# A relational graph layer: who fetches the message rows, which engine copies, and how wide the one-hot products are

## The chip, the cores and the metric

The kernel runs on one core of a Trainium2 chip. The metric is the device time of one execution in microseconds (us), the median of several runs. A core has five engines with instruction queues of their own: TensorE (PE), VectorE (DVE), ScalarE (ACT), GpSimd (POOL) and SyncE (SP). Each works through its queue in order, and semaphores tie them together. Transfers are issued by SP, ACT or POOL and carried out by DMA engines.

## The reference

There are N = 12500 nodes with 256 features and E = 212500 edges, sorted by destination, among them one loop edge per node, which is the last edge of its node. Each edge has one of R = 8 types.

```python
h = jnp.maximum(_layernorm(x, axis=-1), 0.0)
hx = jnp.einsum('ni,rio->rno', h, weight)            # (8, 256, 256) weights
agg = jax.ops.segment_sum(hx[edge_type, src], dst, num_segments=num_nodes)
node_repr = agg * 0.5 ** 0.5 + h_bias
return x + node_repr + (h @ loop_weight) * 0.5 ** 0.5
```

## The kernel before

The kernel first sums rows of h per destination and type, and multiplies by the weights afterwards, once per node and type.

**Norms.** In the first 110 us SP loads x in pieces of 512 rows, DVE and ACT normalise them, and SP writes h to a table in DRAM. Edges taken before that table is complete have rows of x gathered instead, which DVE and ACT normalise in place (kind "x").

**Units and tiles.** Edges are taken in 802 units. The first 128 units (block 0) hold 256 edges each. Later units hold 267 edges, from which the loop edges are squeezed out, so that at most 256 are left. Each unit is two tiles of 128 edges, 1603 tiles in all. Blocks of 128 units are prepared together on DVE (`prepare`): source numbers (`gidx`), window columns (`col`), and, for some tiles, source addresses in bytes (`single`). Which half of a unit a tile holds is told by `place_of`.

**Gathers.** For tile t, `gather` (L739) puts an indirect DMA on POOL's queue (L755): 128 rows of 1 KB into a buffer `msg`, one edge per partition. It is put down AHEAD = 58 tiles before the tile is used; there are 60 tile buffers, in pairs. Every SINGLE-th tile (t%48 = 47, from block 1 on) is not gathered by POOL: `load_sources` (L759) loads 16 addresses into registers of SP (L762), and SP then issues one DMA per row (L767). The list `fetches` spreads these steps: it begins HOLD = 8 tiles after the tile was put down, and `fetch` takes FETCH = 4 of them per tile.

**Sums.** DVE builds one-hot matrices (L785), 176 columns per edge: 22 window nodes times 8 types. PE multiplies rows by one-hots (L818), two matrix products per tile, each as two matmuls of fp32, and adds a unit's two tiles in one PSUM bank. REACH gives offset and width, in nodes, of each tile's window: 22 nodes for the first tile of a unit (176 columns), 18 from node 4 on for the second (144 columns). `add_sums` (L832, DVE) adds the bank to a ring of accumulators `acc` in SBUF, at an offset in a register. There are four banks.

**Nodes.** Groups of 128 nodes follow when their sums are complete: 32 matmuls with the weights plus 4 with the loop weight (L1009), spread over the tiles by a planner that counts DVE credits, then two additions (L1021, L1022) and an output store by SP (L1027). For a group to come, PE turns rows of h into `pt` (L859), DVE writes the loop edges' part of the accumulators (L881, eight operations), and ACT copies `pt` to `self_t` (L864). Every fourth group, the types of the loop edges are found: marks (L902, DVE), a matmul, `kinds`, four `diagonal` products on ACT (L934), a matmul that spreads them, and a copy to `types` on ACT (L945).

The program order within each queue is written out by the Python loop over t; nothing reorders it.

Of the kernel before, what the change touches and what calls it, by code (L numbers as in the profile page):

```python
# [13 lines left out]
AF = mybir.ActivationFunctionType  # L14
ALU = mybir.AluOpType
# [3 lines left out]
SYNC_DEP = mybir.DependencyInfo(mybir.DependencyClass.Sync, mybir.DependencyReason.DATA)  # L19
DVE = mybir.EngineType.DVE  # L20
SP = mybir.EngineType.SP

P = 128
EPS = 1e-5
# [3 lines left out]
XG = 4  # L28
# [4 lines left out]


WIN = 22
REACH = ((0, 22), (4, 18))

GROUP = 128

# [4 lines left out]
MSGS = 60  # L44
AHEAD = 58

SINGLE = 48
FETCH = 4
SOURCES = 16
HOLD = 8  # L50


# [167 lines left out]
def kernel(  # L220
# [54 lines left out]

    def place_of(t):
        u, i = divmod(t, PAIR)
        return u // P, i, u % P


    with ExitStack() as main:
# [32 lines left out]
        single, fetches = {}, []  # L314
        state = {"h32": None}


# [39 lines left out]
        def kept_sources(b, got):  # L357

            def keep():
                single[b] = idx.tile([P, P], I32, name="single")  # L360
                nc.vector.tensor_single_scalar(
                    single[b], got["sf"][:, P:U], float(D * 4), op=ALU.mult)

            return [keep]

# [115 lines left out]
        def columns(b, got):  # L481


            halves = [(slice(i * P, (i + 1) * P), o, n) for i, (o, n) in enumerate(REACH)]

            def bases():
                if b == 0:
# [16 lines left out]
                        got["there"][:, h], got["col"][:, h], float(o), None, op0=ALU.is_ge)  # L504

            def plain_to():
                nc.vector.scalar_tensor_tensor(
                    got["there"][:, :U], got["col"][:, :U], float(WIN), got["there"][:, :U],
                    op0=ALU.is_lt, op1=ALU.mult)

            def plain_typed():
                nc.vector.scalar_tensor_tensor(
# [226 lines left out]
        def gather(t):  # L739
            if t % PAIR == 0:  # L740
                both = msgs.tile([P, PAIR, D], F32, name="msg")
                for i in range(PAIR):
                    msg[t + i] = both[:, i, :]
            if t % QUAD:
                kind[t] = kind[t - 1]
            else:
                kind[t] = "h" if state["h32"] is not None and t >= state["h32"] + LATE else "x"
            table = {"h": h32, "x": x}[kind[t]]
            b, i, u = place_of(t)
            if b and i and kind[t] == "h" and t % SINGLE == SINGLE - 1 and t + AHEAD < NT:  # L750
                for r in range(0, P, SOURCES):
                    fetches.append((done["tile"] + HOLD, lambda r=r: load_sources(t, r)))
                return
            at = i * P + u
            nc.gpsimd.indirect_dma_start(  # L755
                out=msg[t], out_offset=None, in_=table[:, :],
                in_offset=bass.IndirectOffsetOnAxis(ap=gidx[b][:, at : at + 1], axis=0))

        def load_sources(t, r0):  # L759

            b, _, u = place_of(t)
            _, vals = nc.values_load_multi_w_load_instructions(  # L762
                single[b][u : u + 1, r0 : r0 + SOURCES], engines=[SP],
                min_val=0, max_val=(N - 1) * D * 4,
                skip_runtime_bounds_check_because="clamped to the table where they are computed")
            for i, v in reversed(list(enumerate(vals))):
                fetches.insert(0, (0, lambda i=i, v=v: nc.sync.dma_start(  # L767
                    msg[t][r0 + i : r0 + i + 1, :].bitcast(U8),
                    h32_bytes[:, bass.ds(v, D * 4)])))

        def fetch(n):
            for _ in range(n):
                if fetches and fetches[0][0] <= done["tile"]:
                    fetches.pop(0)[1]()

        def onehots(t):

            n = min(QUAD, NT - t)
            o = ohs.tile([P, QUAD // PAIR, PAIR, C], F32, tag="oh", name="oh")
            b, _, u = place_of(t)  # L780
            k = 0
            for v, i in ((n // PAIR, PAIR), (1, n % PAIR)):
                if v and i:
                    of = col[b].rearrange("p (i u) -> p u i", i=PAIR)[:, u + k : u + k + v, :i]
                    j = nc.vector.tensor_tensor(  # L785
                        o[:, k : k + v, :i, :],
                        iota_f.unsqueeze(1).unsqueeze(1).to_broadcast([P, v, i, C]),
                        of.unsqueeze(3).to_broadcast([P, v, i, C]), op=ALU.is_equal)
                    k += v
            for i in range(n):  # L790
                oh[t + i] = o[:, i // PAIR, i % PAIR, :]
                made[t + i] = j.ins.name

        def load_offsets(u0):
# [8 lines left out]
        def edge_sums(t):  # L803
            m, o = msg.pop(t), oh.pop(t)
            if t % PAIR == 0:
                bank = banks[t // PAIR % BANKS]
                sums["ps"] = bank[:, : KC * R * WIN].rearrange("p (c k) -> p c k", c=KC)
            ps = sums["ps"]
            i = t % PAIR
            from_, width = (a * R for a in REACH[i])  # L810
            end = t == NT - 1 or i == PAIR - 1
            free = added.get(t // PAIR - BANKS)
            if i == 0 and free is not None and latest["pe"] is not None:
                tc.add_manual_dep(latest["pe"], free.name, SYNC_DEP, reason="bank is free")
            if i == 0 and latest["pe"] is not None:
                tc.add_manual_dep(latest["pe"], made[t], SYNC_DEP, reason="one-hots are made")
            for c in range(KC):
                j = nc.tensor.matmul(  # L818
                    ps[:, c, from_ : from_ + width], m[:, c * P : (c + 1) * P], o[:, :width],
                    start=(i == 0 and c == 0), stop=(end and c == KC - 1))  # L820
            latest["pe"] = j.ins
            return ps
# [28 lines left out]
        def turn_nodes(g, pool, written=None):  # L851

            n = plan.ends[g] - plan.starts[g]
            pst = pt[:, : KC * P].rearrange("p (c d) -> p c d", c=KC)

            def turn():
                rows_ = got["h", g // XG][:, g % XG, :]
                for c in range(KC):
                    nc.tensor.transpose(  # L859
                        pst[:, c, :n], rows_[:n, c * P : (c + 1) * P], ident[:n, :n])  # L860

            def keep():
                got["self", g] = pool.tile([P, KC, GROUP], F32, name="self_t")
                i = nc.scalar.activation(got["self", g][:, :, :n], pst[:, :, :n], AF.Copy)  # L864
                if written:
                    tc.add_manual_dep(
                        i.ins, written[0].name, SYNC_DEP, reason="one reader at a time")

            return turn, keep, pst

        def begin(g):

            n = plan.ends[g] - plan.starts[g]
            q, k = divmod(g, XG)
            written = []
            turn, keep, pst = turn_nodes(g, selves, written)
            s0 = g % SLOTS * GROUP

            def own(r):
                of = typed[q][:, k * GROUP : k * GROUP + n].unsqueeze(1).to_broadcast([P, KC, n])  # L880
                i = nc.vector.scalar_tensor_tensor(  # L881
                    acc[:, :, r, s0 : s0 + n], of, float(r + 1), pst[:, :, :n],
                    op0=ALU.is_equal, op1=ALU.mult)
                if r == R - 1:
                    zeroed[g, "slot"] = i.ins
                    written.append(i.ins)
# [20 lines left out]
        def find_types(q):  # L907
# [11 lines left out]
            def kinds_of():  # L919
# [27 lines left out]
            shared(spread, [(1, types_of)], lambda: q in marked, wait=2)  # L947

        got = {}

# [14 lines left out]
        def group_ahead(g):  # L965
# [11 lines left out]
            if q < plan.typed:  # L977
                def turned_nodes():
                    turn, keep, _ = turn_nodes(g, early)
                    shared(turn, [(1, keep)])  # L980

                work.append((0.4, turned_nodes))
            if k == XG - 2:
# [286 lines left out]
```

## Time and profile before

Times are in us.

| what | value |
|---|---|
| median of 3 runs | 2020.09 (2018.17 to 2021.71) |
| profiled execution: time, span | 2023.05, 2021.3 |
| PE, busy | 1796.2 |
| DVE, busy | 1317.4 |
| ACT, busy | 218.4 |
| POOL, busy | 1500.7 |
| gathers from h / from x | 1480 / 96 |
| rows fetched one by one by SP | 3456 |
| matmuls of 176 / 144 columns (L818) | 3208 / 3204 |
| granted TensorE clock, mean | 0.957 |

A group line gives source line, engine, operation, written tile <- read tiles, shape, count, then busy time and the mean duration of one. A timeline line gives start, duration, engine, line and operation, and in brackets the idle time before it with what ended it. A line of busy time by stage gives the stretch, its length, busy time with the number of instructions for PE's matmuls and weight loads, then granted clock, DMA share and GB/s. A line of waits gives who waited for whom, the total, the number and the longest. SPq is SP's sequencer, which issues DMAs. Durations under a source line are minimum/median/maximum in ns.

### The profile page before, as it was taken

How to read it: one execution, taken by the hardware profiler on the slowest of the kernel's cores; microseconds unless marked ns; L12 is line 12 of the kernel's file. 1: busy time of each engine (PE TensorE's matmuls, PEld its weight loads, DVE VectorE, ACT ScalarE, POOL GpSimd, SP SyncE). 2: the span in 40 equal slices, each digit the busy share in tenths (PEclk: the TensorE clock that was granted, in tenths of full speed). 3: DMA queues.
4: the chain of work that ended last, by engine and by line, in shares of the span. 5: the costliest groups of instructions: out<-in, count | busy, mean ns of one | idle time of the engine just before them, and what ended most of it. 6: DMA issues, size and time to landing. Idle time of an engine off the chain costs nothing.

```text
span 2021.3 us, 36386 instructions
## 1 busy us (share of the span) xinstructions
PE 1796.2 (89%) x10411; PEld 1610.0 (80%) x10411; DVE 1317.4 (65%) x3281; ACT 218.4 (11%) x470; POOL 1500.7 (74%) x1602
## 2 busy tenths in 40 slices
PE   2468999997999898999899999998998898998998
PEld 2357999997888888988788788787787787787886
DVE  7869566687656578656577655577665568665642
ACT  7854110000000000000000000000000000000000
POOL 7766777777777777777777777777777777777773
PEclk8569999998999999999999999999999999999999
DMA  8973443444444444444444444444444444444442
GB/s 296 380 222 97 146 138 106 128 138 127 129 139 118 139 137 117 130 118 139 130 126 139 128 124 135 132 122 140 129 118 138 125 123 129 118 138 123 118 120 73
DMA packets 152577, 281.63 MB, mean 139 GB/s; under 512 B 31149, under 2 KB 101940, under 8 KB 152372
## 3 DMA queue, kind: packets, MB, share of 16 engines
q0 software_dynamic: 75648, 206.67, 35.1%
q1 hardware_dynamic: 76724, 72.61, 11.4%
q8 instruction: 82, 1.34, 0.3%
q14 instruction: 123, 1.01, 0.2%
HBM read 253.55 MB, written 25.60 MB: 138 GB/s over the span
## 4 chain that ended last, share of the span: by engine, by line
PE 38%; DMA 20%; SPq 17%; issue 12%; POOL 7%; DVE 5%; ACT 2%; DVEq 0%; POOLq 0%; ACTq 0%
PE ps L818 20%; PE po L1009 17%; DMA msg<-h,gidx 13%; SPq L767 13%; POOL msg L755 7%; SPq L762 4%; DMA hr<-h 2%; DMA h<-xt 1%; DVE e_stats L701 1%; DVE acc L832 1%; ACT xt L713 1%; DMA xr<-in_x_dram 1%; DMA w<-in_L_gnn_weight_dram 1%; DMA msg<-h 1%; DVE oh L785 1%
## 5 line engine op out<-in xcount | busy, mean ns | idle before, releaser
L755 POOL DMA_INDIRECT msg<-h,gidx x1480 | 1407.7, 951 | 464.2 <-issue 371.1
L818 PE MATMUL ps<-oh,msg 128*128 128x176 f32 (+1 forms) x6412 | 1169.6, 312 | 201.5 <-DMA msg<-h,gidx 78.5
L818 PEld LDWEIGHTS ps<-oh,msg 128*128 128x128 f32 x6412 | 1037.8, 196 | 355.3 <-DMA msg<-h,gidx 159.1
L1009 PE MATMUL po<-w,acc 128*128 128x256 f32 x3136 | 883.0, 383 | 1.8 <-DVE acc L832 1.8
L832 DVE TENSOR_TENSOR acc<-acc,ps 128x352 f32 x802 | 415.1, 518 | 503.4 <-PE ps L818 499.1
L1009 PEld LDWEIGHTS po<-w,acc 128*128 128x128 f32 x3136 | 537.6, 192 | 25.3 <-DVE acc L832 2.6
L785 DVE TENSOR_TENSOR oh<-fixed,cols 128x704 f32<-128x704 f32 x402 | 353.0, 879 | 0.0
L881 DVE SCALAR_TENSOR_TENSOR acc<-types,pt 128x256 f32<-128x256 bf16 (+1 forms) x688 | 249.0, 411 | 77.5 <-PE pt L859 71.5
L864 ACT ACTIVATE self_t<-pt 128x256 f32<-128x256 f32 x98 | 37.5, 383 | 1456.4 <-DVE acc L881 1352.5
L755 POOL DMA_INDIRECT msg<-in_x_dram,gidx x96 | 91.0, 948 | 31.1 <-issue 24.4
L1009 PE MATMUL po<-wl,self_t 128*128 128x256 f32 x392 | 105.2, 391 | 4.9 <-ACT self_t L864 2.5
L1009 PEld LDWEIGHTS po<-wl,self_t 128*128 128x128 f32 x392 | 69.1, 196 | 11.4 <-ACT self_t L864 2.9
L1021 DVE TENSOR_TENSOR xr<-xr,po 128x256 f32<-128x256 f32 x98 | 40.5, 413 | 17.5 <-PE po L1009 15.7
L713 ACT ACTIVATE xt<-xt,n_shift,n_rstd 128x256 f32<-128x256 f32 x98 | 50.9, 588 | 8.6 <-DVE n_shift L710 8.6
L713 ACT ACTIVATE msg<-msg,e_shift,e_rstd 128x256 f32<-128x256 f32 x96 | 49.6, 589 | 12.8 <-DVE e_shift L710 12.8
L1022 DVE TENSOR_TENSOR xr<-xr,po 128x256 f32<-128x256 f32 x98 | 41.2, 420 | 3.4
L934 ACT ACTIVATE diagonal<-ident,kinds 128x128 bf16<-128x128 f32 x88 | 28.1, 390 | 135.0 <-DVE kinds L931 130.1
L859 PE MATMUL pt<-ident,hr 128*128 128x128 f32 x196 | 37.9, 275 | 0.0
L370 DVE TENSOR_SCALAR moves<-fixed 128x267 int32<-128x267 int32 x84 | 36.0, 428 | 1.1
L701 DVE BATCH_NORM_STATS2 n_stats<-xt 128x6 f32<-128x256 f32 x98 | 34.4, 412 | 2.5 <-DMA xt<-in_x_dram 1.7
L371 DVE COPY_PREDICATED fixed<-moves,fixed 128x266 int32<-128x266 int32 (+6 forms) x84 | 33.7, 401 | 2.9
L701 DVE BATCH_NORM_STATS2 e_stats<-msg 128x6 f32<-128x256 f32 x96 | 33.5, 411 | 0.0
(201 smaller groups left out, 319.7 us busy)
## 6 DMA issues: line engine op xcount, KB each, us to landing
msg<-h SPq DMA_DIRECT2D x3456, 1.0 KB
msg<-h,gidx POOLq DMA_INDIRECT x1480
xt<-in_x_dram SPq DMA_DIRECT2D x24, 512.0 KB
h<-xt SPq DMA_DIRECT2D x24, 512.0 KB
xr<-in_x_dram SPq DMA_DIRECT2D x24, 512.0 KB
hr<-h SPq DMA_DIRECT2D x24, 512.0 KB
out_dram<-xr SPq DMA_DIRECT2D x24, 512.0 KB
w<-in_L_gnn_weight_dram SPq DMA_DIRECT2D x2, 1024.0 KB
```

Source lines behind the costliest of these rows:

```text
L701: nc.vector.bn_stats(stats[:n, j, :], rows_[j])
L713: nc.scalar.activation(rows_[j], rows_[j], AF.Relu, bias=shift[:n, j : j + 1], scale=rstd[:n, j : j + 1])
L755: nc.gpsimd.indirect_dma_start(out=msg[t], out_offset=None, in_=table[:, :], in_offset=bass.IndirectOffsetOnAxis(ap=gidx[b][:, at : at + 1 ...
L762: _, vals = nc.values_load_multi_w_load_instructions(single[b][u : u + 1, r0 : r0 + SOURCES], engines=[SP], min_val=0, max_val=(N - 1) * D ...
L767: fetches.insert(0, (0, lambda i=i, v=v: nc.sync.dma_start(msg[t][r0 + i : r0 + i + 1, :].bitcast(U8), h32_bytes[:, bass.ds(v, D * 4)])))
L785: j = nc.vector.tensor_tensor(o[:, k : k + v, :i, :], iota_f.unsqueeze(1).unsqueeze(1).to_broadcast([P, v, i, C]), of.unsqueeze(3).to_broa ...
L818: j = nc.tensor.matmul(ps[:, c, from_ : from_ + width], m[:, c * P : (c + 1) * P], o[:, :width], start=(i == 0 and c == 0), stop=(end and ...
L832: i = nc.vector.tensor_tensor(a, a, ps, op=ALU.add)
L881: i = nc.vector.scalar_tensor_tensor(acc[:, :, r, s0 : s0 + n], of, float(r + 1), pst[:, :, :n], op0=ALU.is_equal, op1=ALU.mult)
L1009: i = nc.tensor.matmul(got["out", g][:n], lhs, rhs, start=(r == R and c == 0), stop=(r == R - 1 and c == KC - 1))
L1021: nc.vector.tensor_add(rows_[:n, k, :], rows_[:n, k, :], outs[g % 2][:n, 1, :])
L1022: nc.vector.tensor_add(rows_[:n, k, :], rows_[:n, k, :], got["out", g][:n])
```

## The change

It does these things:

- SINGLE goes from 48 to 32, so that one tile in 32 is fetched row by row. Its rows are shared: runs of 32 rows (SOURCES) go in turn to SP and ACT, each with a list of its own, and FETCH = 3 steps per tile are taken from each list.
- `self_t` and `types` are copied by DVE instead of ACT, and the four `diagonal` products on ACT become one operation on DVE. The extra dependency that kept ACT behind DVE's last reader of `pt` goes.
- The two halves of a unit change places: PE takes the second half of the edges first, at 176 columns, and then the first half, in a window of 13 nodes from node 0 (104 columns, before 144). In the last block both halves have 176 columns.

```diff
+ACT = mybir.EngineType.Activation
-REACH = ((0, 22), (4, 18))
+REACH = ((0, 13), (0, 22))
-SINGLE = 48
-FETCH = 4
-SOURCES = 16
+SINGLE = 32
+FETCH = 3
+SOURCES = 32
     def place_of(t):
         u, i = divmod(t, PAIR)
-        return u // P, i, u % P
+        half = 0 if PAIR * u + 1 == NT else PAIR - 1 - i
+        return u // P, half, u % P
...
-                    single[b], got["sf"][:, P:U], float(D * 4), op=ALU.mult)
+                    single[b], got["sf"][:, :P], float(D * 4), op=ALU.mult)
...
-            if b and i and kind[t] == "h" and t % SINGLE == SINGLE - 1 and t + AHEAD < NT:
-                for r in range(0, P, SOURCES):
-                    fetches.append((done["tile"] + HOLD, lambda r=r: load_sources(t, r)))
-                return
+            if b and t % PAIR and kind[t] == "h" and t + AHEAD < NT:
+                if t % SINGLE == SINGLE - 1:
+                    for k, r in enumerate(range(0, P, SOURCES)):
+                        engine = (SP, ACT)[k % 2]
+                        fetches[engine].append((
+                            done["tile"] + HOLD,
+                            lambda r=r, engine=engine: load_sources(t, r, engine)))
+                    return
...
         def fetch(n):
-            for _ in range(n):
-                if fetches and fetches[0][0] <= done["tile"]:
-                    fetches.pop(0)[1]()
+            for list_ in fetches.values():
+                for _ in range(n):
+                    if list_ and list_[0][0] <= done["tile"]:
+                        list_.pop(0)[1]()
...
-            from_, width = (a * R for a in REACH[i])
+            width = R * (REACH[0][1] if i and t // (PAIR * P) < NB - 1 else WIN)
...
-                    ps[:, c, from_ : from_ + width], m[:, c * P : (c + 1) * P], o[:, :width],
+                    ps[:, c, :width], m[:, c * P : (c + 1) * P], o[:, :width],
...
-                i = nc.scalar.activation(got["self", g][:, :, :n], pst[:, :, :n], AF.Copy)
-                if written:
-                    tc.add_manual_dep(
-                        i.ins, written[0].name, SYNC_DEP, reason="one reader at a time")
+                nc.vector.tensor_copy(got["self", g][:, :, :n], pst[:, :, :n])
...
-                for g in range(XG):
-                    nc.scalar.activation(
-                        marked[q][:, g * GROUP : (g + 1) * GROUP], ident, AF.Copy,
-                        scale=kinds[:, g : g + 1])
+                nc.vector.tensor_tensor(
+                    marked[q].rearrange("p (g k) -> p g k", g=XG),
+                    ident.unsqueeze(1).to_broadcast([P, XG, GROUP]),
+                    kinds.unsqueeze(2).to_broadcast([P, XG, GROUP]), op=ALU.mult)
...
-                nc.scalar.activation(typed[q], pt, AF.Copy)
+                nc.vector.tensor_copy(typed[q], pt)
```

The copies of `types` and of the first groups' `self_t` are also placed one tile later in the program. The preparation of window columns follows the new REACH; it writes one more operation for block 0.

More of the change, by code (lines that the diff above doesn't have):

```diff
@@ L313 @@
         added, zeroed = {}, {}
-        single, fetches = {}, []
+        single, fetches = {}, {SP: [], ACT: []}
         state = {"h32": None}
@@ L481, in columns @@
         def columns(b, got):
-            halves = [(slice(i * P, (i + 1) * P), o, n) for i, (o, n) in enumerate(REACH)]
+            halves = [(slice(i * P, (i + 1) * P), o, n)
+                      for i, (o, n) in enumerate(REACH if b < NB - 1 else ((0, WIN), (0, WIN)))]
             def bases():
@@ L506, in plain_to @@
             def plain_to():
-                nc.vector.scalar_tensor_tensor(
-                    got["there"][:, :U], got["col"][:, :U], float(WIN), got["there"][:, :U],
-                    op0=ALU.is_lt, op1=ALU.mult)
+                for h, o, n in halves:
+                    nc.vector.scalar_tensor_tensor(
+                        got["there"][:, h], got["col"][:, h], float(o + n), got["there"][:, h],
+                        op0=ALU.is_lt, op1=ALU.mult)
             def plain_typed():
@@ L757, in gather, with load_sources @@
                 in_offset=bass.IndirectOffsetOnAxis(ap=gidx[b][:, at : at + 1], axis=0))
-        def load_sources(t, r0):
+        def load_sources(t, r0, engine):
             b, _, u = place_of(t)
             _, vals = nc.values_load_multi_w_load_instructions(
-                single[b][u : u + 1, r0 : r0 + SOURCES], engines=[SP],
+                single[b][u : u + 1, r0 : r0 + SOURCES], engines=[engine],
                 min_val=0, max_val=(N - 1) * D * 4,
                 skip_runtime_bounds_check_because="clamped to the table where they are computed")
+            queue = {SP: nc.sync, ACT: nc.scalar}[engine]
             for i, v in reversed(list(enumerate(vals))):
-                fetches.insert(0, (0, lambda i=i, v=v: nc.sync.dma_start(
+                fetches[engine].insert(0, (0, lambda i=i, v=v: queue.dma_start(
                     msg[t][r0 + i : r0 + i + 1, :].bitcast(U8),
@@ L790, in onehots @@
             for i in range(n):
-                oh[t + i] = o[:, i // PAIR, i % PAIR, :]
+                oh[t + i] = o[:, i // PAIR, place_of(t + i)[1], :]
                 made[t + i] = j.ins.name
@@ L849, in clear, with turn_nodes @@
             zeroed[g, "slot"] = i.ins
-        def turn_nodes(g, pool, written=None):
+        def turn_nodes(g, pool):
             n = plan.ends[g] - plan.starts[g]
@@ L874, in begin @@
             q, k = divmod(g, XG)
-            written = []
-            turn, keep, pst = turn_nodes(g, selves, written)
+            turn, keep, pst = turn_nodes(g, selves)
             s0 = g % SLOTS * GROUP
@@ L885, in own @@
                     zeroed[g, "slot"] = i.ins
-                    written.append(i.ins)
             def write():
@@ L944, in types_of @@
                 typed[q] = types.tile([P, XG * GROUP], BF16, name="types")
-                nc.scalar.activation(typed[q], pt, AF.Copy)
-            shared(spread, [(1, types_of)], lambda: q in marked, wait=2)
+                nc.vector.tensor_copy(typed[q], pt)
+            shared(spread, [(2, types_of)], lambda: q in marked, wait=2)
         got = {}
@@ L979, in turned_nodes @@
                     turn, keep, _ = turn_nodes(g, early)
-                    shared(turn, [(1, keep)])
+                    shared(turn, [(2, keep)])
                 work.append((0.4, turned_nodes))
```

## The prediction

> **What bounds the kernel now.** I read the page's shares first, then instructions by shape, GpSimd's timeline, busy time by stage, and the waits. The shares of the page name no bound:
>
> ```profile
> PE 1796.2 (89%) x10411; PEld 1610.0 (80%) x10411; DVE 1317.4 (65%) x3281; ACT 218.4 (11%) x470; POOL 1500.7 (74%) x1602
> ```
>
> POOL is 74% busy, but its timeline (start, duration, idle before) has no free time:
>
> ```profile
> 999.76 0.95 POOL L755 DMA_INDIRECT msg<-h,gidx  x1 [0.30 <-issue]
> ...
> 1001.01 0.95 POOL L755 DMA_INDIRECT msg<-h,gidx  x1 [0.30 <-issue]
> ...
> 1002.26 0.95 POOL L755 DMA_INDIRECT msg<-h,gidx  x1 [0.30 <-issue]
> ```
>
> A gather takes 0.95 us, the next starts 0.30 us later, and this 0.30 is put down to issue: one gather per 1.252 us. POOL makes 1576 of them (96 from x, 1480 from h), beginning at 4.75 us:
>
> ```profile
> 4.75 1.11 POOL L755 DMA_INDIRECT msg<-in_x_dram,gidx  x1 [2.11 <-DVE bound_o L1085]
> ...
> 135.13 0.94 POOL L755 DMA_INDIRECT msg<-h,gidx  x1 [0.30 <-issue]
> 140.96 0.95 POOL L755 DMA_INDIRECT msg<-h,gidx  x1 [4.89 <-issue]
> ...
> 1995.42 1.17 POOL L755 DMA_INDIRECT msg<-h,gidx  x1 [0.30 <-issue]
> ```
>
> 1576 x 1.252 = 1973 us. The gaps over 0.30 us, all between 128 and 200 us, add 12.9 us. Some 34 gathers that lasted 1.0 to 1.26 us add about 7 us. Within 1 us that accounts for the 1992 us from the first gather to the end of the last at 1996.6; a tail of 24.8 us follows, to the span of 2021.3.
>
> That PE has slack shows in its own rate by stage (matmuls of L818; four make one tile of 128 edges):
>
> ```profile
> 200.00:300.00 100.00, 65.66 (x385) 61.11 (x386) 1.00 0.49 142
> ...
> 500.00:600.00 100.00, 60.02 (x338) 55.83 (x337) 0.95 0.44 127
> ...
> 1200.00:1300.00 100.00, 59.65 (x325) 50.73 (x324) 0.98 0.45 131
> ```
>
> PE eats 96 tiles in 100 us while the 58 tiles gathered ahead last, 84 in the middle, and from about 1050 us 81, which is POOL's 80 or 81 gathers of each such stretch plus the fetched tiles. The waits name what holds it: between 400 and 600 us the rows that SP fetches, between 1200 and 1600 us the gathers:
>
> ```profile
> PE ps L818 <- DMA msg<-h: 17.2, 3, 10.4
> ```
> ```profile
> PEld ps L818 <- DMA msg<-h,gidx: 63.9, 92, 2.8
> PE ps L818 <- DMA msg<-h,gidx: 32.2, 44, 2.4
> ```
>
> So PE outruns POOL, is then held by SP, and at last waits for each gather. SP's delay costs nothing in the end, because POOL never stops for it and PE must meet POOL anyway. The end is set by the number of gathers times 1.252 us. The page's chain, which gives PE 38%, hides this: it counts PE's work between two gathers as PE's.
>
> **The change part by part.**
>
> *Gathers.* A fetched tile was t%48 = 47 from tile 287 to 1535, 27 of them (3456 row DMAs / 128). With t%32 = 31 it is 40. POOL has 1480 - 13 = 1467 gathers from h. 13 x 1.252 = **-16.3 us**, on the path.
>
> *Row fetches.* SP's lines show one fetched tile's price:
>
> ```profile
> L767 SPq DMA_DIRECT2D msg<-h x3456: 224/228/1088, 343.7 to 1906.4; - x192
> ```
> ```profile
> 486.27 1.29 SPq L762
> 492.85 1.29 SPq L762
> ```
>
> From one load of 16 addresses to the next is 6.58 us: 1.29 for the load and 16 rows of 0.33. A tile took 8 x 6.58 = 52.6 us on SP; with SP's large DMAs (0.4 to 0.5 us each) and their waits that is the 57 us per 48 tiles at which PE runs in the middle. Now SP and ACT each issue 64 rows per fetched tile, 21.1 us, and two loads of 32 addresses. No row shows a load of 32; between one and two loads of 16 each it is 2.6 to 5.2 us for the pair. So 24 to 26 us on each engine, while POOL gives 31 gathers in 38.8 us: a third of the queue is free. The step FETCH = 3 spreads a tile over 22 program tiles (66 entries), after HOLD = 8, and the tile is used 58 after it was put down, so 28 tiles, some 34 us, of margin remain. SP's output stores wait for DVE (up to 21.6 us between 1000 and 2000 us) and rows queue behind them: that fits in the margin. On ACT, once the early norms and clears are done (about 255 us), only row fetches and one load of the flag are left, so nothing that PE needs queues behind them. Cost taken 0. No row shows a DMA issued by ACT; its price is taken from the nearest, SP's 0.33 us, and it counts once it passes (38.8 - 5.2) / 64 = 0.525 us. A gain from it is excluded, since POOL sets the pace.
>
> *ACT's copies on DVE.* ACT loses 98 self_t (37.5 us), 88 diagonals (28.1) and 22 types (13.1). DVE gains 98 copies at 0.424 us (the nearest row, L351's copy of 128x256 from pt), 41.6 us; 22 types and 22 diagonals of 128x512 at 0.68 us (between 0.424 for 256 and 0.879 for 704 elements), 30 us. DVE goes from 1317 to about 1389 us, 69%: 0.87 us per tile against POOL's 1.21. Behind each copy on DVE wait the sums of the bank and the one-hots, hence PE; four banks and one-hots made eight tiles ahead cover 0.7 us, and if not, PE's slack does. From about 200 us on this is 0. Before 200 us DVE is 80% busy and its chain paces PE, which delays POOL's buffers (the 12.9 us). Four copies fall there: +1.7 us if all add up; or -2.5 us if PE's wait for ACT's self_t at 136 us goes. I take +0.5, near the middle.
>
> *What the DVE work does to POOL.* The long gathers are not random. This one lies beside two mark instructions of L902:
>
> ```profile
> 1310.90 0.48 DVE L902 TENSOR_SCALAR mark<-line,firsts 128x512 bf16<-128x512 f32 x1
> 1311.00 1.20 POOL L755 DMA_INDIRECT msg<-h,gidx  x1 [0.30 <-PE ps L818]
> ```
>
> Over the trace the 54 marks go with 0.11 us of longer gather each, operations on two SBUF tensors (L435, L440, L563, L989) with 0.03 to 0.16, those reading PSUM with next to nothing. The new diagonal reads two SBUF tensors (ident, kinds): 22 x 0.1 = **+2.2 us**, at most 22 x 0.32 (the longest stretch) = 7.0, at least 0. The copies read PSUM: 0.
>
> *Narrower matmuls.* In the unthrottled stretch matmuls follow each other after 149 ns at 176 columns, 122 at 144 and 216 at 256, so 0.84 ns a column; 104 columns make 88, or stay at 122 if the weight load does not get shorter. 768 pairs x 4 x 34 ns = 104 us less PE work, or none; in the last block 34 pairs grow from 144 to 176, 3.7 us. All of it lies under POOL's 1.252. In the tail PE is busy, but there the widths are the last block's: +0.2 at most, taken as 0.
>
> **Sum:** -16.3 + 2.2 + 0.5 = -13.6 us. The profiled execution took 2023.05 (span 2021.3 and 1.75 around it) and would take 2009.4; it stands 3.0 above the median 2020.09, so the median becomes 2006.5. Measurement can tell about 0.2%, 4 us.
>
> **The rivals.**
>
> *Slower: ACT's row costs more than SP's.* Nothing in the trace shows an ACT-issued DMA. The point is 0.525 us a row. At twice SP's price, 0.66, a fetched tile takes ACT 47.4 us; the fortieth would be ready at 344 + 40 x 47.4 = 2240, 68 tiles at PE's 1.02 us and the tail follow: about **2330 us**. For it: two engines feed one set of DMA engines at once. Against it: these move at 45% of their time, and a row's issue looks like the issuing engine's own work, 0.228 us plus a register move. 0.09.
>
> *Gain eaten: diagonals hold POOL for their whole length.* 22 x 0.68 = 15 us instead of 2.2: -16.3 + 15 + 0.5, **2019.3**, within noise; with the 98 copies stretching gathers by 0.11 each, another 10.8, **2030**. For it: the marks' stretches; against it: the mean stretch, a fifth of an instruction's length, and L351's copies, which show none worth naming. The Trainium skill (SBUF — State Buffer, Who interferes with whom) states that a DVE instruction with two SBUF inputs contends with a GpSimd instruction that reads SBUF, and that the port is held for the whole instruction; by that rule it is 2019.3, by the row 2006.5; the trace agrees that they meet, not on the length. 0.07 for 2019.3, 0.04 for 2030.
>
> *More: POOL's early stalls go too*, because narrower matmuls free buffers sooner: -16.3 - 12.9 + 2.2, **1993**. Against it: PE waits there for ACT's norms and DVE's sums, not for itself. 0.03.
>
> *The change doesn't do what it says:* were an edge of a first half outside 13 columns, the counts would differ and the general path would run, far slower. Worked out from the reference's inputs, the greatest column of a first half is 10 and of a second 19. 0.01.
>
> **How the numbers follow.** The forecast has 0.76; its own bounds are 1999 (-18.8 and the runs' 2 us) to 2013 (+7.0, +1.7). The range goes from 1998 to 2021, to take in the eaten gain; out of it stay 0.09 + 0.04 + 0.03 + 0.01 = 0.17. Faster 0.76 + 0.03 = 0.79, same 0.07, slower 0.14.
>
> **What would show it.** POOL: 1467 gathers from h, still 1.25 us apart, last one near 1983 us. PE waits for rows of h (45.5 us now) gone; tiles per 100 us above 90 until the 58 ahead are used up, well before 1050 us, then about 82.5. ACT's rows near 0.33 us. DVE near 1389 us. It is wrong if gathers lie further apart than 1.262 us, or if PE waits for rows to the end.

## The result and the profile after

The changed kernel takes 2030.74 us (median of 16 runs, 2022.5 to 2041.43), the kernel before, run beside it, 2019.18 (16 runs): a ratio of 1.0056, 95% interval 1.0046 to 1.0067. It is slower by half a per cent, where 2006.5 in a range of 1998 to 2021 was forecast. The profiled execution took 2029.05, with a span of 2027.3 and a mean granted clock of 0.933.

Half of the prediction came true. This is the page's line of engine shares, then GpSimd's group and its last gathers in the timeline (start, duration, idle before):

```profile
PE 1750.0 (86%) x10411; PEld 1596.6 (79%) x10411; DVE 1373.5 (68%) x3424; ACT 140.3 (7%) x262; POOL 1489.9 (73%) x1589
```
```profile
L763 POOL DMA_INDIRECT msg<-h,gidx x1467 | 1396.9, 952 | 459.4 <-issue 362.3
```
```profile
1978.86 0.95 POOL L763 DMA_INDIRECT msg<-h,gidx  x1 [0.30 <-issue]
1980.11 0.95 POOL L763 DMA_INDIRECT msg<-h,gidx  x1 [0.30 <-issue]
```

There are 1467 gathers, still 1.25 us apart, and the last ends at 1981.1 (1983 was forecast; 1996.6 before). But the span goes on for 46.3 us after it, where before it went on for 24.8. POOL gained 15.5 us and no longer sets the end. What does, the chain of waits says (shares of the span by line):

```profile
DMA msg<-h 28%; PE ps L828 18%; PE po L1014 16%; DMA msg<-h,gidx 6%; ACTq L776 4%; POOL msg L763 3%; SPq L776 2%; ACTq L770 2%; ACT xt L717 1%; DMA h<-xt 1%; DVE acc L842 1%; DVE e_stats L705 1%; DMA hr<-h 1%; DMA xr<-in_x_dram 1%; DVE oh L795 1%
```

The first entry, transfers of h into `msg` without `gidx`, are the rows fetched one by one: 28% of the chain, and before 1%. The gathers (with `gidx`) fell from 13% to 6%. PE's matmuls by stage (busy us and number, weight loads, granted clock, DMA share, GB/s) answer to those of the prediction:

```profile
200.00:300.00 100.00, 63.80 (x392) 60.84 (x391) 1.00 0.48 142
500.00:600.00 100.00, 56.62 (x331) 50.35 (x332) 1.00 0.45 132
...
1200.00:1300.00 100.00, 54.49 (x324) 52.15 (x323) 0.93 0.44 130
1300.00:1400.00 100.00, 44.38 (x264) 42.81 (x264) 0.86 0.44 128
1600.00:1700.00 100.00, 47.23 (x280) 45.67 (x280) 0.87 0.43 125
```

PE began as foretold (98 to 100 tiles per 100 us while the 58 gathered ahead last), then fell, from 1000 us on, to 71, 66 and 70 tiles in some stretches of 100 us, below POOL's 80; in others it caught up, with at most 90 (360 matmuls / 4 between 1400 and 1500 us). The waits name two reasons, one for PE and one for DVE (total, number, longest):

```profile
PE ps L828 <- DMA msg<-h: 87.7, 18, 11.3
...
DVE rise L389 <- DMA nat_d<-in_dst_dram: 54.4, 4, 23.3
```

Both come out of one queue. This is SP's timeline where the longest of them lies, then the DVE instruction that waited, then PE in steps of 10 us (busy us and matmuls, granted clock):

```profile
1351.67 23.15 SPq L776 DMA_DIRECT2D msg<-h  x46
1375.02 0.37 SPq L338 DMA_DIRECT2D nat_s<-in_src_dram  x1
1375.76 0.37 SPq L338 DMA_DIRECT2D nat_d<-in_dst_dram  x1
```
```profile
1378.10 0.44 DVE L389 TENSOR_TENSOR rise<-nat_d 128x267 f32<-128x267 int32 x1 [23.28 <-DMA nat_d<-in_dst_dram]
```
```profile
1350.00:1360.00 10.00, 10.00 (x71) 1.00 0.48 148
1360.00:1370.00 10.00, 2.58 (x17) 0.89 0.38 109
1370.00:1380.00 10.00, 0.00 (x0) 0.50 0.52 151
1380.00:1390.00 10.00, 7.85 (x41) 0.76 0.50 155
1390.00:1400.00 10.00, 9.69 (x60) 1.00 0.39 112
```

The loads of the next block's indices stood in SP's queue behind 46 rows that took 23.15 us, 0.50 each. DVE, in order, waited 23.28 us for them with its sums and diagonals behind, and PE stood still for 19.6 us (7.4 + 10.0 + 2.2 of the three middle steps). The clock follows the pause: 0.50 while PE idles, 0.76 in the step in which it resumes, so the pause costs a little even after it has ended. The Trainium skill (TensorE: Matmul & The Clock Gate, Part 1) says that the gate goes to half after an idle window of about 3.4 us and opens again after a busy one; the two 10 us steps of this trace agree.

### The profile page after: what moved, and what is told of

It reads as the page before. It is cut to its first block, busy times and chain, and to the rows that moved or that the text cites. A ratio compares the mean times of both kernels' runs of the same rounds, so it can differ in the third digit from the quotient of the medians.

```text
span 2027.3 us, 39592 instructions
## 1 busy us (share of the span) xinstructions
PE 1750.0 (86%) x10411; PEld 1596.6 (79%) x10411; DVE 1373.5 (68%) x3424; ACT 140.3 (7%) x262; POOL 1489.9 (73%) x1589
## 4 chain that ended last, share of the span: by engine, by line
DMA 38%; PE 35%; issue 7%; ACTq 6%; DVE 5%; POOL 3%; SPq 3%; ACT 2%; DVEq 0%; POOLq 0%
DMA msg<-h 28%; PE ps L828 18%; PE po L1014 16%; DMA msg<-h,gidx 6%; ACTq L776 4%; POOL msg L763 3%; SPq L776 2%; ACTq L770 2%; ACT xt L717 1%; DMA h<-xt 1%; DVE acc L842 1%; DVE e_stats L705 1%; DMA hr<-h 1%; DMA xr<-in_x_dram 1%; DVE oh L795 1%
## 5 line engine op out<-in xcount | busy, mean ns | idle before, releaser
L828 PE MATMUL ps<-oh,msg 128*128 128x176 f32 (+1 forms) x6412 | 1112.8, 304 | 209.8 <-DMA msg<-h 87.7
L1014 PE MATMUL po<-w,acc 128*128 128x256 f32 x3136 | 900.1, 389 | 0.8 <-DVE acc L842 0.8
L1026 DVE TENSOR_TENSOR xr<-xr,po 128x256 f32<-128x256 f32 x98 | 40.5, 413 | 17.3 <-PE po L1014 15.5
L874 DVE COPY self_t<-pt 128x256 f32<-128x256 f32 x98 | 40.8, 417 | 3.2 <-PE pt L869 3.2
L389 DVE TENSOR_TENSOR rise<-nat_d 128x267 f32<-128x267 int32 x6 | 2.6, 434 | 54.4 <-DMA nat_d<-in_dst_dram 54.4
L946 PE MATMUL pt<-diagonal,ones_b 128*128 128x512 bf16 x22 | 8.7, 398 | 32.6 <-DVE diagonal L938 32.6
L869 PEld LDWEIGHTS pt<-ident,hr 128*128 128x128 f32 x196 | 26.1, 155 | 12.9 <-DVE types L950 12.8
```

Of the source, the lines that this page charges most:

```text
L828: j = nc.tensor.matmul(ps[:, c, :width], m[:, c * P : (c + 1) * P], o[:, :width], start=(i == 0 and c == 0), stop=(end and c == KC - 1))
L869: nc.tensor.transpose(pst[:, c, :n], rows_[:n, c * P : (c + 1) * P], ident[:n, :n])
L874: nc.vector.tensor_copy(got["self", g][:, :, :n], pst[:, :, :n])
L1014: i = nc.tensor.matmul(got["out", g][:n], lhs, rhs, start=(r == R and c == 0), stop=(r == R - 1 and c == KC - 1))
```

## What a row costs when two engines fetch

**Where the rows' time goes.** These are SP's waits ahead of its rows, first of the kernel before, then of the changed one, and then the rows' and the loads' own durations after (minimum/median/maximum in ns):

```profile
SPq L767 <- DMA msg<-h: 0.7, 3, 0.4
```
```profile
SPq L776 <- DMA msg<-h: 356.7, 710, 8.6
```
```profile
L776 ACTq DMA_DIRECT2D msg<-h x2560: 213/213/793, 340.8 to 1896.5; - x197
L776 SPq DMA_DIRECT2D msg<-h x2560: 224/228/835, 340.9 to 1922.9; - x197
...
L770 ACTq TENSOR_LOAD <-single x80: 2171/2322/3912, 253.5 to 1879.9; - x80
L770 SPq TENSOR_LOAD <-single x80: 2106/2223/3702, 290.9 to 1910.5; - x80
```

A row costs ACT no more than SP (213 and 228 ns). What is new is 357 us in which SP waits for an earlier row to land; before, it was 0.7 us. Each of these DMAs reports its landing on one of eight semaphores, which the DMAs of SP and ACT share, and it waits on that same semaphore before it is issued. In the kernel before, the last DMA on it was, for all 3456 rows, SP's own, eight places earlier in SP's queue. With two engines that take semaphores alternately, the engine's own last DMA on the semaphore lies four places earlier for 1596 of SP's 2560 rows and 1644 of ACT's. Of these, 1254 and 1383 start within 0.15 us of the last landing recorded on their semaphore; of the 3456 rows before, 61 did. A row lands 1.81 us (median) after its issue starts. Eight rows at 0.323 us take 2.58 us, longer than the 1.66 us of the landing before, so SP never waited; four take 1.29, so now both engines do. Four per landing is 1.81 / 4 = 0.45 us a row.

The changed trace holds its own comparison. Where a row follows a row on the same engine, the mean distance between the two is:

| semaphore last used by the engine's own DMA | SP | ACT |
|---|---|---|
| eight places earlier | 0.355 us (320 rows) | 0.333 us (229) |
| four places earlier | 0.469 us (1573) | 0.483 us (1626) |
| all such rows | 0.467 us (2448) | 0.462 us (2479) |

Rows with eight places behave as before (0.346), but most of them fall where the other engine issues nothing, so the other engine's traffic could be the cause instead. Rows before which the other engine had issued none for 1.5 us tell the two apart: on SP 0.423 us with four places (184 rows) against 0.352 with eight (245), on ACT 0.484 (215) against 0.318 (141). So the places slow the queue without that traffic. The traffic adds something too: with two or more rows of the other engine in these 1.5 us, eight places take 0.415 (25 rows) and 0.410 (39), four 0.476 and 0.479 (1348 each). A row's landing went from 1.66 to 1.81 us.

**One fetched tile on SP.** From SP's first row to its last are 1582 us for 40 tiles, 39.6 us each: 64 rows one after the other 28.6 (1142.6 / 40), stretches with a load of addresses 6.4, and stretches with SP's large DMAs 4.6. The 31 gathers between two fetched tiles take 38.8. The queue is too slow by 2%, and there is no third of it free. PE's start on a fetched tile less the issue of the last row of SP's share is below 2.5 us, hence about a landing, at 17 of the 40 tiles; ACT's share was there 14 to 54 us ahead of PE at every one.

## Experiments: which part makes it slower

Theory S, formed from the traces: rows of both engines share one chain of eight completions, which makes them too slow for one tile in 32. Rival C: the copies on DVE hold the work back and cost the time. For the last four runs theory B and rival W ask which of the other parts turns the rows' gain into a loss: the copies or the windows.

Each kernel ran beside the kernel before, and ratios are to it. In the four comparisons of this section, made side by side, it took 2019.91 us (31 runs).

**h1: the rows alone.** The kernel before with this edit only:

```diff
-SINGLE = 48
-FETCH = 4
-SOURCES = 16
+SINGLE = 32
+FETCH = 3
+SOURCES = 32
...
+                    engine = (SP, ACT)[k % 2]
```

> The kernel before with the row part alone (one fetched tile in 32, SyncE and ScalarE, 32 rows in turn; copies, diagonals and windows as before). Theory S (rows of both engines share one chain of eight completions; about 39.4 us per fetched tile, against 38.8 us of gathers): where the kernel before takes 2019, this is slower, 2025 to 2045, with PE waiting for rows after 1000 us and the last gather near 1980. Rival C (the copies moved to VectorE hold SyncE's loads back and cost the time): 2002 to 2012, faster than before. Where the kernel before takes 2590: about 2550 by both, as twice before.

Measured: 2012.75 us, 0.9967 (0.9956 to 0.9979), faster. Theory S, as it was stated, fell, and C's range was just missed. Yet rows matter here too. These are the chain by line, ACT's wait for rows, SP's, and PE's wait for ACT's copies:

```profile
DMA msg<-h 32%; PE ps L824 14%; PE po L1015 14%; ACTq L772 6%; SPq L772 5%; DMA xr<-in_x_dram 3%; ACTq L766 2%; DMA hr<-h 2%; DMA h<-xt 1%; DVE acc L838 1%; ACT xt L714 1%; DVE e_stats L702 1%; DVE oh L791 1%; DMA msg<-h,gidx 1%; DMA w<-in_L_gnn_weight_dram 1%
```
```profile
ACT self_t L870 <- DMA msg<-h: 961.7, 53, 36.5
```
```profile
SPq L772 <- DMA msg<-h: 336.6, 661, 5.7
```
```profile
PE pt L921 <- ACT self_t L870: 95.3, 17, 12.2
```

The last gather ends at 1977.8 and 32.4 us follow, 7.6 more than before: part of the gain goes back to the rows. But SP's last row is issued at 1894.1 (1922.9 in the changed kernel), every share of rows is 17 to 37 us ahead of PE, and DVE does not wait for `nat_d`. Two things differ. First, 1333 of SP's rows and 1340 of ACT's have a semaphore four places back, 263 and 304 fewer; at the 0.11 us between the table's first two lines that is an estimate of 30 us on SP. The stretches of row after row took 20.5 us less (1122.1 against 1142.6), and SP's rows end 28.8 us earlier. Second, PE waits for ACT's `self_t`, which queues behind ACT's rows, so PE runs less far ahead of them: 73 tiles in 400 to 500 us, where the changed kernel takes 96.

**h2: all but the rows.** The changed kernel with SINGLE = 48, FETCH = 4, SOURCES = 16 and

```diff
-                        engine = (SP, ACT)[k % 2]
+                        engine = SP
```

> The changed kernel with SyncE alone, one in 48 and 16 rows in turn as before; copies on VectorE and the narrow windows stay. Theory S: the loss goes, 2016 to 2024 where the kernel before takes 2019 (POOL again bound by 1576 gathers). Rival C: the loss stays, 2026 to 2040 at least, since all copies are still on VectorE. Where the kernel before takes 2590: about 2585 by both.

Measured: 2021.86 us, 1.001 (1.0001 to 1.002). The copies on DVE and the windows cost 0.1% by themselves. Rival C falls.

**h3 and h4: fewer fetched tiles.** The changed kernel with one number different:

```diff
-SINGLE = 32
+SINGLE = 40
```

> The changed kernel with one fetched tile in 40 (33 tiles or 32, against 40 and 27). Theory S: 39.4 us per fetched tile fits into 39 x 1.252 = 48.8 us of gathers, PE no longer waits for rows late in the run, POOL sets the end again: about 6 gathers fewer than before, 2010 to 2017 where the kernel before takes 2019, faster than both kernels. Rival C: as slow as the change, 2028 to 2036. Where the kernel before takes 2590: 2515 to 2530, between one in 36 and one in 48.

> The changed kernel with one fetched tile in 48, the number of before. Theory S: rows are ready well ahead (39.4 us against 58.8), the gathers are as many as before, 2016 to 2023 where the kernel before takes 2019. If the early waits for rows (400 to 600 us) cost nothing, equal to before; rival C: 2030 to 2040. Where the kernel before takes 2590: about 2510, as before.

Measured: one in 40 gives 2016.07 us, 0.9978 (0.9968 to 0.9987); one in 48 gives 2020.72, 1.0003 (0.9993 to 1.0012). Both are as theory S had them. With 40, a fetched tile may take 48.8 us of gathers, and rows and gathers keep step (47.9 a tile on SP, 1533.3 / 32). PE's weight loads then wait for gathers, and rows are 2% of the chain:

```profile
PEld ps L828 <- DMA msg<-h,gidx: 226.9, 337, 3.6
```
```profile
PE ps L828 23%; PE po L1014 20%; DMA msg<-h,gidx 18%; POOL msg L763 9%; DMA msg<-h 2%; DVE acc L842 1%; DMA msg<-in_x_dram,gidx 1%; ACTq L776 1%; DVE oh L795 1%; ACT xt L717 1%; DMA h<-xt 1%; DVE e_stats L705 1%; SPq L776 1%; PE pt L869 1%; DVE moves L372 1%
```

The tail after the last gather is 25.4 us with 40 and 25.8 with 48, as the 24.8 of before. So the loss needs both halves: the rows at one in 32, and copies or windows in their new places. Take either back and it is gone; give the rows a little more time and it is gone as well.

## Experiments where rows set the pace from the start

In the other four comparisons the kernel before itself took 2572 to 2600 us, and the trace of g1 shows steps of some 0.7 us between instructions of SP, POOL and PE again and again; why, no run shows. Each is compared only with the kernel before beside it. They show the same parts under another balance: SP alone needed 74.5 us per fetched tile (57.6 otherwise), where 47 gathers at 1.252 us take 58.8, so rows were late before the change, and a second engine for them is a gain. Expectations that speak of 2019 us alone miss for that reason.

**g1, g2, g3: the two kernels, and one in 36.** g1 is the kernel before, g2 the changed one, g3 the changed one with `SINGLE = 36`.

> The kernel before itself, for its trace beside the others on the same chip. Where it takes 2019 us its trace should be the one known: gathers 1.252 us apart throughout, SP's rows 0.33 us apart. Where it takes 2590 us, as beside the last runs, all theories expect that something lengthens the steps between instructions on every engine's queue, SP's rows first: about 75 us per fetched tile in place of 57.6, so that rows and not gathers set the pace.

> The changed kernel itself beside it. Theory S, where the kernel before takes 2019: 2027 to 2034, as known, with 39 to 40 us per fetched tile. Where it takes 2590: rows set the pace there already before the change, at 75 us per 48 tiles of SP alone; two engines in one window of eight need 45 to 50 us per 32 tiles, much the same per tile, and the 13 gathers fewer count little: 2545 to 2580. Theory L: slower than before there too, above 2600.

> The changed kernel with one fetched tile in 36: 35 fetched tiles, 8 gathers fewer than before. Theory S, where the kernel before takes 2019: gathers leave 35 x 1.252 = 43.8 us per fetched tile and the window needs 39 to 40, so the gathers set the end: -10.0 + 2 for stretched gathers, 2009 to 2014, faster than both kernels. Theory D or L: 2027 to 2036. Where the kernel before takes 2590: 2510 to 2550, by the rows' lower rate.

Measured: g1 one run of 2576.42; g2 0.9848 (0.9815 to 0.9881), 49.1 us per fetched tile (1962.1 / 40) instead of 74.5; g3 0.9788 (0.9752 to 0.9823). PE's waits for rows in g1 are nearly four times the 45.5 us of the profile before:

```profile
PE ps L818 <- DMA msg<-h: 166.3, 20, 14.8
```

**e1, e2, e3 and f1, f2: one in 48, rows alone, rows undone.** The same kernels as h4, h1 and h2; f1 repeats e3, f2 repeats e2.

> The changed kernel with one fetched tile in 48 in place of 32; all else stays. Theory S (shared window): the row DMAs of SP and ACT take eight completion semaphores in turn, in program order, and each waits for the landing of the DMA eight before it; so the two engines together need 39.4 us per fetched tile, while at one in 32 the gathers leave only 38.8. At one in 48 they leave 47 x 1.252 = 58.8 us, so the waits for rows vanish, the gathers (1480 from h again) set the end, and the time is 2019 + 2 for gathers stretched by the diagonals: 2018 to 2024. Theory D (the copies and diagonals on DVE, or the order of the halves, cost the time): the loss stays and 13 gathers come back, 2035 to 2048.

> The kernel before with the row part of the change alone: one tile in 32, SP and ACT in turn with 32 rows each, three steps per tile; the copies stay on ACT and the windows are as before. Theory S: the loss comes with it, 2025 to 2050, the upper part because ACT's copies now queue behind rows that wait. Theory D: only the 13 gathers saved remain, 2001 to 2008.

> The changed kernel with the row part undone: one tile in 48, SP alone, 16 rows a load, four steps per tile; copies on DVE and the narrow windows stay. Theory S: no loss, and no gain since gathers set the end: 2017 to 2024 (the diagonals' stretching is worth +2). Theory D: the whole loss and 13 more gathers: 2035 to 2048.

> Asked again, since the kernel before took 2593 us in the first runs. The changed kernel with the row part undone: one tile in 48, SP alone, 16 rows a load, four steps per tile; copies on DVE and the narrow windows stay. Theory S: no loss, and no gain since gathers set the end: 2017 to 2024 where the kernel before takes 2019. Theory D: the whole loss and 13 more gathers: 2035 to 2048.

> Asked again. The kernel before with the row part of the change alone; the copies stay on ACT and the windows are as before. Theory S: the loss comes with it, 2025 to 2050, the upper part because ACT's copies now stand in one queue with rows that wait. Theory D: only the 13 gathers saved remain, 2001 to 2008.

Measured: one in 48 0.9677 (0.9645 to 0.9709); rows alone 0.9849 (0.9816 to 0.9882) and 0.9845 (0.9797 to 0.9892); rows undone 0.9987 (0.9963 to 1.0011) and 0.9968 (0.9944 to 0.9992). Here the rows carry the whole effect of the change, and with two engines fewer fetched tiles are again better.

**e4: a tile to each engine in turn**, and **f3: the lists interleaved row by row.**

```diff
-FETCH = 3
+FETCH = 4
...
-                        engine = (SP, ACT)[k % 2]
+                        engine = (SP, ACT)[t // SINGLE % 2]
```
```diff
-            for list_ in fetches.values():
-                for _ in range(n):
+            for _ in range(n):
+                for list_ in fetches.values():
```

> The changed kernel, but each fetched tile belongs to one engine, SP and ACT by turns, with four steps per tile so that their stretches of the program hardly overlap. Each engine then has 77 us for 128 rows and four loads, about 50 us of its own issuing. Theory S: in program order ACT's rows come after SP's of the tile before and wait for their semaphores, so the two take turns and cannot overlap: 50 to 56 us per fetched tile, 2450 to 2650 us in all. Theory L (rows are slow because two engines issue at once, in the transfers themselves): nothing is shared, 2003 to 2012.

> The changed kernel with the rows of SP and ACT put down one by one in turn, not three by three. Theory S: a window of eight then always holds four rows of each engine, where three and three leave an engine with three at times; each engine can issue four rows per landing of 1.8 us: 37 to 39 us per fetched tile in place of 39.4, about what the gathers leave, and the time falls to 2005 to 2022. Theory L (transfers slowed because two engines issue at once): the same as the changed kernel, 2027 to 2034. A theory of the DVE parts: the same, 2027 to 2034.

Measured: e4 took 2719.96 us in its one run, the slowest of all and above theory S's 2450 to 2650, though each engine has as many rows as in g2 and no tile's rows are shared; 1499 of SP's and 1546 of ACT's rows still have a semaphore four places back. So the semaphores are not given out in the order in which the Python loop lists the rows, as theory S had assumed; why e4 is slower than g2 stays open. f3 is 0.9847 (0.9799 to 0.9895), the changed kernel's ratio, where theory S expected a gain. It tests nothing: each list goes to a queue of its own, whose order the edit leaves as it was, and all 2719 DMAs of SP and 2560 of ACT have the same semaphores as in the changed kernel. f3 is a second run of g2.

**i1 to i4.** i1 is the changed kernel with the three copies back on ACT, i4 with the windows and the order of the halves of before, i2 with the index loads on ACT; i3 is h1 with `SINGLE = 36`. The core of the first three:

```diff
-                nc.vector.tensor_copy(got["self", g][:, :, :n], pst[:, :, :n])
+                i = nc.scalar.activation(got["self", g][:, :, :n], pst[:, :, :n], AF.Copy)
...
-                nc.vector.tensor_copy(typed[q], pt)
+                nc.scalar.activation(typed[q], pt, AF.Copy)
```
```diff
-REACH = ((0, 13), (0, 22))
+REACH = ((0, 22), (4, 18))
```
```diff
-                    nc.sync.dma_start(n[:full, : size + more], bass.AP(
+                    (nc.scalar if b else nc.sync).dma_start(n[:full, : size + more], bass.AP(
```

> The changed kernel with self_t, diagonal and types back on ScalarE; rows of two engines, one in 32, and the narrow windows stay. h1 (rows alone) took 0.9967 of before and the whole change 1.0056, so the copies or the windows turn the gain into the loss. Theory B (ScalarE's copies, which stand in its queue among the rows and which PE waits for, kept PE from running ahead of the rows; without them PE runs into SyncE's rows and into late index loads): 2008 to 2015, as h1, where the kernel before takes 2019. Rival W (the other order of the halves and the windows make the rows late): 2026 to 2034, as the whole change.

> The changed kernel with the windows and the order of the halves of before; rows of two engines, one in 32, and copies on VectorE stay. Theory B: 2024 to 2034, the loss is there without the windows. Rival W: 2008 to 2015.

> The changed kernel with the loads of the next 4272-edge block's indices (nat_s, nat_d, nat_t) issued by ScalarE, whose rows are 30 to 50 us ahead of PE, where SyncE's are 2 to 6 us ahead. Theory B with late loads as its main part: VectorE's waits of 54.4 us for nat_d go and with them 10 us or more, 2012 to 2022. Theory B with the rows as its main part: PE then waits for rows instead, 2026 to 2032.

> The kernel before with the row part alone, but one fetched tile in 36 (36 of 40 tiles). Rows of h1 came every 38.8 us against 38.8 us of gathers, so at 36 the gathers allow 43.8 us and have the last word again: 9 gathers fewer than before, 11 us off: 2006 to 2012 where the kernel before takes 2019, and the tail from the last gather to the end back at 25 us from 32.4. If ScalarE's copies behind rows set h1's pace by themselves: 2012 to 2018.

Measured: i1 0.9846 (0.9806 to 0.9887), i4 0.9794 (0.9761 to 0.9828), i2 0.9736 (0.9706 to 0.9767), i3 0.9743 (0.9711 to 0.9775). The times do not answer B against W, since under this balance rows are late in every variant. The traces do say which part changes the chaining of the rows, because the semaphores are fixed when the program is built (g2 has the changed kernel's for all 5279 DMAs, at another pace). Four places back are 1303 and 1315 rows (SP, ACT) in i1, as in h1, and 1625 and 1669 in i4, as in the changed kernel: it goes with the copies' engine, not with the windows. i2 gains 1.1% on g2's ratio, another comparison, by taking three loads per block out of SP's queue.

What stays open: how the changed kernel's loss divides between the more chained rows, the late index loads and PE's running ahead without ACT's copies. The kernels that would divide it (i1, i2, i4) were not run where the kernel before takes 2019 us. Nor was the number of semaphores varied, or the places by themselves; that landing and places set the spacing rests on the traces.

## Why the prediction was wrong, step by step

- **Gathers, right.** 13 fewer moved POOL's end by 15.5 us; 16.3 - 2.2 - 0.5 = 13.6 was forecast. A few us of this are the spread of single traces: in h2, with none fewer, POOL ended 5.1 us earlier (1991.5).
- **Row fetches, the step that failed.** It said "24 to 26 us on each engine, while POOL gives 31 gathers in 38.8 us: a third of the queue is free", and took the cost as 0. SP needed 39.6. Against the middle of the forecast, 21.1 + 3.9 = 25.0, the rows are 7.5 longer (28.6), the loads 2.5 (6.4), and 4.6 are SP's large DMAs, which were counted for the kernel before and then left out. The distance between rows alone decides: with 0.33 in place of 0.467, 61 times, the tile would have taken 31 us and fitted.
- **Its price per row** came from SP running alone, where 0.33 is the issue; with two engines it is the landing that counts. The same trace held the warning: a landing of 1.66 us against 8 x 0.323 = 2.58.
- **Its point of decision** was 0.525 us a row, with nothing but loads beside the rows. With the 11.0 us per tile that go to loads and large DMAs, and 61 distances left, it is (38.8 - 11.0) / 61.2 = 0.454, and 0.467 lies just above. Hence half a per cent, not the 2330 us of the rival that had two engines and slow rows; its reason, ACT's dearer row, is refuted by 213 against 228 ns.
- **"That fits in the margin"** overlooked that rows also hold up what stands behind them: the index loads, DVE's 54.4 us. The prediction asked what delays the rows in SP's queue, not whom the rows delay.
- **"From about 200 us on this is 0"** for ACT's copies holds alone (h2, 0.1%), but not with the rows: SP has 1596 chained rows with the copies on DVE and 1303 with the same kernel's copies on ACT (i1), and PE lost what kept it from running ahead (argued from h1's waits, not tried by itself).
- **Diagonals, right in kind, the size by luck.** Gathers stretched by 8.6 us after 215 us, 7.0 before: +1.6, forecast +2.2. But the diagonals' own part is 3.4 us, and it is not spread evenly. A gather that begins while a diagonal runs is longer by what is left of the diagonal, less 0.13 us: this one, of 0.95 us otherwise, by 0.38, with 0.51 left.

```profile
471.26 0.69 DVE L938 TENSOR_TENSOR diagonal<-ident,kinds 128x512 bf16<-128x512 f32 x1
471.44 1.33 POOL L763 DMA_INDIRECT msg<-h,gidx  x1 [0.30 <-issue]
```

  So it is in 11 of the 13 gathers that begin within a diagonal (0.04 to 0.45 us each); the other two begin in its last 0.12 us. A gather that is already running when a diagonal begins is not lengthened (942 to 947 ns in 14 of 15 cases). The Trainium skill (SBUF — State Buffer, SBUF: two separate sides) has the pair of ports that DVE and GpSimd share as an exclusive lock, which whoever starts first gets for the whole instruction, and the trace agrees. So the prediction's "not on the length" was a misreading: the gather that it shows at 1311.00 began with 0.38 us of a mark left and took 0.25 us longer. The rival's 15 us did not come because only 13 of 22 diagonals had a gather begin in them, and each cost the rest alone. A diagonal takes 0.693 us, a `types` copy 0.689 (0.68 each forecast), and DVE is at 1373.5 instead of 1389.
- **Narrow matmuls**, off the path, as said: of a tile's four the second follows the first after 89 ns, near the 88 forecast, the third and fourth after 112.
- **What would show it wrong** was named: "if PE waits for rows to the end". It does, 58.1 us of it between 1000 and 1600 us and 27.2 after that (17.3 + 9.9).

The Trainium skill (DMA: Bandwidth & Descriptors, Issuing engines are not separate DMA queues) says that issuing on several engines at once "will only save the time on the sequencer it takes to initiate the DMA". This case agrees, and adds how much: two engines took 0.233 us a row together (0.467 / 2), where one took 0.346, not half of it.

## What to carry to other kernels

For a stream of small DMAs, compare issue time times the number of completion semaphores with the landing time: by these traces an engine alone may be bound by issue, and two engines that share the semaphores by the landing. Where two producers feed one consumer at rates that differ by a few per cent (39.6 against 38.8 us here), choose the share with a margin: one in 40 gave 0.9978 where one in 32 with the same copies gave 1.0056, and rows alone gave 0.9967. Before a queue is filled, look at what stands behind it and at what its consumer was held back by.

## What the hardware showed unexpectedly

- A load of 32 addresses into an engine's registers takes 2.22 us on SP and 2.32 on ACT, one of 16 takes 1.26: it goes with the number.
- fp32 matmuls of 144 columns start every 122 ns, of 176 every 149, of 256 every 216; of 104 columns the second of a tile's four starts 89 ns after the first, but the third and fourth after 112. What sets this pace besides the columns, no run shows.
- A gather pays for a DVE operation on two SBUF tensors only if it begins while that one runs, and then for all that is left of it but 0.13 us (11 gathers beside diagonals, 3.4 us in all).
- A row's landing hardly noticed a second issuing engine (1.66 to 1.81 us); the distance between rows did (0.346 to 0.467 us).
